# A hybrid attention and expert kernel: one written order from the end of the attention on, and all second experts dense

## The chip, the cores and the metric

The kernel runs on one core of one Trainium2 chip. A core has engines that run side by side, each taking its own instructions in order: TensorE (PE in the profile, with its weight loads as PEld), VectorE (DVE), ScalarE (ACT), GpSimd (POOL) and SyncE (SP), which here only issues transfers. The metric is the device time of one execution in microseconds; of several executions the median is given.

## The reference

`x` has four batches of 1024 tokens with 128 features. All is float32. Four stages follow each other, each added to `x` after a layer norm:

```python
x = x + attn_a(layernorm(x))      # 16 heads of 64, causal, softmax with the row's maximum over all columns
x = x + ffn(layernorm(x))         # 32 experts of 128x128, the two best of each token
x = x + attn_b(layernorm(x))      # linear attention: cumulative sums of k*v and k, 16 heads of 8
x = x + ffn(layernorm(x))         # the same experts and router again

# ffn
rw = softmax(x @ router_w.T)                       # (tokens, 32)
vals, idx = top_k(rw, 2)
w_masked = zeros_like(rw).at[tokens, idx].set(vals)
out = sum over e of (x * w_masked[:, e]) @ expert_weights[e]
```

A token needs only its two best experts. A kernel may compute all 32 for every token, with a weight of zero for the other 30 ("dense"), or sort the tokens by expert first and compute only what is needed ("sparse").

## The kernel before

The residual stream `x_sb` stays on the chip as 32 chunks of 128 tokens, 8 to a batch. Four neighbouring chunks are called a quad here.

**The attention** (lines 487 to 845) works through 4 batches x 8 pairs of heads in an order that is written out by hand: within `tc.manual_schedule()`, each engine gets its instructions in the order in which the program emits them. Beside it runs the *sparse* first expert layer of batches 0, 1 and 2: the generator `experts` (from line 214), of which `beside` takes a step in each slot. It sorts tokens with counts on POOL, scatters rows to DRAM with indirect transfers, reads them back sorted, multiplies tile by tile, and writes results to DRAM. Then come 16 indirect transfers per batch (line 449) that POOL issues and that add rows of the results into `x_sb`. They lie in `queue` and are taken out one at a time. The sparse layer of batch 2 is nearly done when the attention ends: one of its 16 additions has been issued then, and 15 are left.

**The stages behind the attention.** The weights of all 32 experts are loaded to `we_sb` (line 856, four transfers of 512 KB). `moe` (line 860) is the dense expert layer, used twice: as "f" for the first expert layer of batch 3 (quads 6 and 7), and as "s" for the second expert layer of batches 1 to 3 (quads 2 to 7). For one quad it does

1. `normed_T` (line 130): statistics unless `known`, the normalised rows `xn` (DVE), four transposes (PE), a copy `xnT` (ACT),
2. the router: four small products `pl` (L886), maximum, `exp`, sum, the two best by `max` and `match_replace` (L892 to L912, mainly DVE), giving the weights `w`,
3. for each of 4 chunks 8 products `pe` of 128x512 (L922, four experts each). Groups 1, 4 and 6 go to ACT: four multiplications by the weight into a tile `t` (L930). The other five go to DVE: four instructions each that multiply and add into `x_sb` (L937). POOL adds the three `t` (L944) and folds the sum (L945, L946); DVE adds that to `x_sb` (L871, in `settle`).

A product lies in one of five PSUM banks (`ps_e`), so PE can be five products ahead of the engine that empties them.

**Who orders what.** `moe` is outside the manual sections: there the compiler's planner orders the instructions of each engine by its own estimate of when each is ready, and it may put them among those of a neighbouring stage, the linear attention included. Between two products `moe` calls `between`: in "f" this is `fill`, which steps the generator `prepare` (L970; norm, projections and feature maps of a quad for the linear attention) for quads 0 and 1, and after turn 8 takes the left-over transfers from `queue`. In "s" it is `pieces`, which steps the *sparse* second expert layer of batch 0 (`experts` with the prefix `s0`; its sums come into tiles `y_s` and are added to `x_sb` by DVE, L476 and L481).

**The linear attention** (from L1071) is manual. For each chunk `u`, POOL forms the products `kv` (L1085), PE sums them over the chunk (`cum`, L1103) and carries them on (L1111), DVE multiplies by the queries (`m`, L1123) and reduces (`num`, L1132), and `finish` transposes, projects and adds to `x_sb` (L1152). `ahead` steps `prepare` for quads 2 to 7.

Of the kernel before, what the change touches and what calls it, by code (L numbers as in the profile page):

```python
# [15 lines left out]
P = 128  # L16
# [4 lines left out]
def hybrid_kernel(  # L21
# [107 lines left out]

    def normed_T(pool, xnp, c0, n, nm, known=None):  # L130

        mv, rstd = known or statistics(c0, n, nm)
        xn = xnp.tile([P, n, D], F32, tag=f"xn{n}", bufs=8 // n, name=f"xn_{nm}")
        xnT = xnp.tile([P, n * P], F32, tag=f"xnT{n}", name=f"xnT_{nm}")
        for c in range(n):
            nc.vector.tensor_scalar(
                xn[:, c, :], x_sb[:, c0 + c, :], mv[:, c, 0:1], rstd[:, c : c + 1],
                ALU.subtract, ALU.mult,
            )
        for g in range(0, n, 4):  # L140
            pt = pool.tile([P, 512], F32, tag="ps1", name=f"pxn_{nm}_{g}")
            for c in range(4):
                nc.tensor.transpose(pt[:, c * P : (c + 1) * P], xn[:, g + c, :], ident)
            nc.scalar.copy(xnT[:, g * P : (g + 4) * P], pt)
        return xnT
# [711 lines left out]
    TB = 12  # L857
    ACT_GROUPS = (1, 4, 6)

    def moe(nm_, store, first=0, between=None, known=(), lag=0):  # L860
        with ExitStack() as ph:
            xnp = ph.enter_context(tc.tile_pool(name=f"xnp{nm_}", bufs=2, reuse_waits="tile"))
            mp = ph.enter_context(tc.tile_pool(name=f"mp{nm_}", bufs=3, reuse_waits="tile"))
            ps_1 = ph.enter_context(tc.tile_pool(name=f"mps1{nm_}", bufs=3, space=PSUM, reuse_waits="tile"))
            ps_e = ph.enter_context(tc.tile_pool(name=f"mpse{nm_}", bufs=5, space=PSUM, reuse_waits="tile"))
            due = []

            def settle(keep):
                while len(due) > keep:
                    xs, s, done = due.pop(0)  # L870
                    nc.vector.tensor_tensor(xs, xs, s[:, :D], ALU.add)  # L871
                    if store and done is not None:
                        b, r = divmod(done, NB)
                        nc.sync.dma_start(
                            out=out_v[b, :, r : r + 4, :], in_=x_sb[:, done : done + 4, :]
                        )

            for q in range(first, NT // 4):
                nm = f"{nm_}_{q}"
                c0 = q * 4  # L880
                xnT = normed_T(
                    ps_1, xnp, c0, 4, f"m{nm}", known[q - first] if known else None
                )
                pl = ps_1.tile([P, 512], F32, tag="ps1", name=f"pl_{nm}")
                for c in range(4):
                    nc.tensor.matmul(  # L886
                        pl[:, c * E : (c + 1) * E], xnT[:, c * P : (c + 1) * P], rwT,
                        start=True, stop=True,
                    )
                plv = pl[:, : 4 * E].rearrange("p (c e) -> p c e", c=4)  # L890
                mx = small.tile([P, 4], F32, tag="mx", name=f"mx_{nm}")
                nc.vector.tensor_reduce(mx, plv, AX.X, ALU.max)  # L892
                ex = mp.tile([P, 4, E], F32, tag="ex", name=f"ex_{nm}")
                nc.vector.tensor_tensor(
                    ex, plv, mx.unsqueeze(2).to_broadcast([P, 4, E]), ALU.subtract
                )
                nc.scalar.activation(ex, ex, AF.Exp)
                sm = small.tile([P, 4], F32, tag="sm", name=f"sm_{nm}")
                nc.vector.tensor_reduce(sm, ex, AX.X, ALU.add)
                nc.vector.reciprocal(sm, sm)  # L900
                tp, rwx = top[q % 2]
                nc.vector.tensor_tensor(
                    rwx[:, :, 0:E], ex, sm.unsqueeze(2).to_broadcast([P, 4, E]), ALU.mult
                )
                m8 = small.tile([P, 4, 8], F32, tag="m8", name=f"m8_{nm}")
                for c in range(4):
                    nc.vector.max(m8[:, c, :], rwx[:, c, 0:E])
                nc.vector.tensor_copy(tp[:, :, 0:2], m8[:, :, 0:2])
                w = mp.tile([P, 4, E + 6], F32, tag="w", name=f"w_{nm}")
                for c in range(4):  # L910
                    nc.vector.match_replace(w[:, c, :], tp[:, c, :], rwx[:, c, :], 0.0)
                nc.vector.tensor_tensor(  # L912
                    w[:, :, 0:E], rwx[:, :, 0:E], w[:, :, 0:E], ALU.subtract
                )
                for c in range(4):
                    xs = x_sb[:, c0 + c, :]
                    parts = []
                    for g in range(E // 4):
                        if between:
                            between(ps_1)  # L920
                        pe = ps_e.tile([P, 512], F32, tag="e", name=f"pe_{nm}_{c}_{g}")
                        nc.tensor.matmul(  # L922
                            pe, xnT[:, c * P : (c + 1) * P],
                            we_sb[:, 4 * g : 4 * g + 4, :].rearrange("p e d -> p (e d)"),
                            start=True, stop=True,
                        )
                        if g in ACT_GROUPS:
                            t = mp.tile([P, 512], F32, tag="t", bufs=TB, name=f"t_{nm}_{c}_{g}")
                            for e in range(4):
                                nc.scalar.mul(  # L930
                                    t[:, e * D : (e + 1) * D], pe[:, e * D : (e + 1) * D],
                                    w[:, c, 4 * g + e : 4 * g + e + 1],
                                )
                            parts.append(t)
                        else:
                            for e in range(4):
                                nc.vector.scalar_tensor_tensor(  # L937
                                    xs, pe[:, e * D : (e + 1) * D],
                                    w[:, c, 4 * g + e : 4 * g + e + 1], xs,
                                    ALU.mult, ALU.add,  # L940
                                )
                    s = parts[0]
                    for t in parts[1:]:
                        nc.gpsimd.tensor_tensor(s, s, t, ALU.add)  # L944
                    nc.gpsimd.tensor_tensor(s[:, :256], s[:, :256], s[:, 256:], ALU.add)  # L945
# [102 lines left out]
    def fill(pool):  # L1048
# [3 lines left out]
        if turn[0] in (4, 18):  # L1052
            preps.append(prepare(len(preps), pool))
# [12 lines left out]
    for p in preps:  # L1066
        for _ in p:
            pass
# [162 lines left out]
```

## Time and profile before

| | us |
|---|---|
| median of 3 runs | 2033.25 (2030.45 to 2037.73) |
| the profiled execution's own time | 2037.51 |
| its span, first to last instruction | 2035.8 |
| attention, to the first transfer of `we_sb` | 0 to 1482 |
| "f", dense first experts of batch 3 | 1482 to 1596.5 (first `cum`) |
| linear attention | 1596.5 to 1785.7 (last addition to `x_sb`) |
| "s", second experts | 1785.7 to 2035.8 |

In the 250 us from 1786 on PE is busy for 213.0 us, DVE for 184.0, POOL for 135.9 and ACT for 102.6. Times in the rows are microseconds from the start of the span. A row of the timeline gives start, length, engine, line, what is written from what, how many instructions were merged, and in brackets how long the engine had been idle and what ended that. Neighbouring instructions of one engine overlap in it, so the length of one is more than what it adds: sixteen instructions of L937 took 4.22 us together, where one alone shows as 0.34.

### The profile page before, as it was taken

Reading aid. Unit: us, or ns where it says so; the run is one execution under the profiler, and the core shown is the slowest. Engines: PE = TensorE matmul, PEld = TensorE weight load, DVE = VectorE, ACT = ScalarE, POOL = GpSimd, SP = SyncE. Lnnn points to the kernel's source line nnn. Section 1 sums busy time; section 2 is a strip of 40 time slices with the busy share of each in tenths; the row PEclk is TensorE's granted clock in tenths of the full one; section 3 lists DMA queues with packets and bytes.
Section 4 is the critical chain, followed back from the end, with each engine's and each line's share of the span. In section 5 each row is a group of like instructions: output and inputs, shape, how many; then the busy total and the mean of one; then the engine's idle time right before and its main releaser. Section 6 shows DMA issues by size and latency. Waiting matters only on the chain.

```text
span 2035.8 us, 33636 instructions
## 1 busy us (share of the span) xinstructions
PE 1890.7 (93%) x10066; PEld 1052.5 (52%) x10066; DVE 1482.9 (73%) x4467; ACT 1234.6 (61%) x3889; POOL 1139.5 (56%) x2080
## 2 busy tenths in 40 slices
PE   6999999999999999999999999999958898987898
PEld 3555555555555655555565555556633454543443
DVE  5777776776787677778767676777547678966788
ACT  4766666676677566766766676776526466334344
POOL 3444445444665476556745854675476566655644
PEclk9999999999999999999999999999979999997999
DMA  7000000000003310000131100003230000004300
GB/s 214 1 1 1 1 1 1 1 1 1 1 13 93 92 22 10 1 1 5 54 107 45 18 1 1 1 17 111 80 82 0 0 0 1 0 1 123 101 11 11
DMA packets 111875, 62.54 MB, mean 31 GB/s; under 512 B 5552, under 2 KB 110160, under 8 KB 111568
## 3 DMA queue, kind: packets, MB, share of 16 engines
q1 hardware_dynamic: 101936, 50.43, 8.7%
q0 software_dynamic: 9472, 8.40, 2.1%
q8 instruction: 82, 1.34, 0.3%
q10 hardware_dynamic: 288, 1.57, 0.2%
q14 instruction: 97, 0.79, 0.1%
HBM read 35.60 MB, written 24.77 MB: 30 GB/s over the span
## 4 chain that ended last, share of the span: by engine, by line
PE 64%; DVE 12%; ACT 10%; POOL 9%; issue 3%; DMA 1%; ACTq 0%; SPq 0%; POOLq 0%; DVEq 0%
PE s L598 19%; PE po L704 10%; PE pt L687 10%; PE pe_s L922 6%; DVE nmx L607 5%; ACT p L632 3%; PE pw L719 3%; PE pk L547 3%; POOL x_sb L449 2%; ACT pT L691 2%; PE pe L430 2%; PE pv L561 2%; PE cum L1103 1%; ACT p L637 1%; PE pe_f L922 1%
## 5 line engine op out<-in xcount | busy, mean ns | idle before, releaser
L607 DVE TENSOR_REDUCE nmx<-s 128x2 f32<-128x1024 f32 x512 | 604.5, 1219 | 218.5 <-PE s L598 217.8
L632 ACT ACTIVATE p<-s,nmx 128x512 f32<-128x512 f32 (+3 forms) x640 | 361.2, 575 | 311.8 <-DVE nmx L607 264.5
L598 PE MATMUL s<-kT,qT 64*128 64x512 f32 x2048 | 518.0, 619 | 8.0 <-ACT p L632 4.5
L674 POOL TENSOR_SCALAR p<-p,f,ri 128x512 f32<-128x512 f32 (+3 forms) x768 | 503.8, 673 | 0.9 <-issue 0.6
L687 PEld LDWEIGHTS pt<-ident,p 128*128 128x128 f32 x2304 | 249.9, 141 | 219.1 <-issue 91.1
L687 PE MATMUL pt<-ident,p 128*128 128x128 f32 x2304 | 335.9, 282 | 24.4 <-POOL rs L652 7.1
L691 ACT COPY pT<-pt 128x512 f32<-128x512 f32 (+3 forms) x768 | 324.4, 510 | 11.9 <-PE pt L687 9.6
L656 POOL TENSOR_TENSOR rs<-rs,f 128x2 f32<-128x2 f32 x256 | 52.1, 204 | 438.5 <-ACT f L623 409.1
L704 PE MATMUL po<-pT,va 128*64 128x256 f32 (+1 forms) x2560 | 291.1, 365 | 0.6 <-DVE oT L711 0.6
L598 PEld LDWEIGHTS s<-kT,qT 64*128 64x128 f32 x2048 | 173.3, 185 | 195.4 <-issue 94.2
L637 ACT ACTIVATE p<-s,nmx 128x128 f32<-128x128 f32 x512 | 180.7, 366 | 107.3 <-DVE nmx L607 104.6
L704 PEld LDWEIGHTS po<-pT,va 128*64 128x64 f32 x2560 | 167.0, 136 | 97.2 <-issue 32.6
L922 PE MATMUL pe_s<-we_sb,xnT_ms 128*128 128x512 f32 x384 | 186.4, 630 | 22.9 <-DVE x_sb L937 16.4
L937 DVE SCALAR_TENSOR_TENSOR x_sb<-pe_s,w_s,x_sb 128x128 f32<-128x128 f32 x480 | 141.4, 343 | 19.2 <-PE pe_s L922 14.6
L645 DVE SCALAR_TENSOR_TENSOR p<-p,qtri 128x128 f32<-128x128 f32 x512 | 144.9, 310 | 7.0 <-ACT p L637 3.9
L652 POOL TENSOR_TENSOR rs<-rs 128x2 f32<-128x2 f32 x192 | 43.9, 229 | 186.7 <-DVE ri L665 186.7
L632 ACT ACTIVATION_READ_ACCUMULATOR p<-s,nmx 128x1 f32 x640 | 139.0, 217 | 0.0
L930 ACT ACTIVATE t_s<-pe_s,w_s 128x128 f32<-128x128 f32 x288 | 82.2, 369 | 92.5 <-PE pe_s L922 75.5
L922 PEld LDWEIGHTS pe_s<-we_sb,xnT_ms 128*128 128x128 f32 x384 | 72.2, 199 | 116.3 <-issue 37.4
L944 POOL TENSOR_TENSOR t_s<-t_s,t_s 128x512 f32<-128x512 f32 x48 | 60.9, 1269 | 81.4 <-ACT t_s L930 81.1
L724 DVE TENSOR_TENSOR x_sb<-pw,x_sb 128x128 f32<-128x128 f32 x128 | 36.9, 289 | 79.8 <-PE pw L719 79.7
L719 PE MATMUL pw<-wo_sb,oT 128*128 128x128 f32 x512 | 84.5, 289 | 1.8 <-DVE x_sb L724 1.0
(302 smaller groups left out, 2669.5 us busy)
## 6 DMA issues: line engine op xcount, KB each, us to landing
xs<-xs_d SPq DMA_DIRECT2D x33, 256.0 KB, 3.1
ys_d<-ys SPq DMA_DIRECT2D x33, 256.0 KB, 2.4
we<-_ffn_expert_weights_dram SPq DMA_DIRECT2D x24, 256.0 KB, 3.6
xs_d<-zero SPq DMA_DIRECT2D x2, 3008.0 KB, 17.9
we<-_ffn_expert_weights_dram SPq DMA_DIRECT2D x45, 64.0 KB, 1.8
xs_s<-xs_d SPq DMA_DIRECT2D x11, 256.0 KB, 3.6
ys_d<-ys_s SPq DMA_DIRECT2D x11, 256.0 KB, 3.4
we_sb<-_ffn_expert_weights_dram SPq DMA_DIRECT2D x4, 512.0 KB, 6.0
```

The source lines that it names most:

```text
L598: nc.tensor.matmul(st[:, h, :], self.qT[rows, self.ib * P : (self.ib + 1) * P], self.kT[rows, j * 512 : (j + 1) * 512], start=True, stop=True,
L607: nc.vector.tensor_reduce(self.nmx[:, i, :], self.s[i], AX.X, ALU.max, negate=True)
L632: nc.scalar.activation(self.p[h][:, at : at + m * P], self.s[i][:, h, : m * P], AF.Exp, bias=bias, accum_out=self.rs[:, i, h : h + 1],)
L637: nc.scalar.activation(self.p[h][:, at + m * P : at + (m + 1) * P], self.s[i][:, h, m * P : (m + 1) * P], AF.Exp, bias=bias,)
L645: nc.vector.scalar_tensor_tensor(d, d, 1.0, qtri, ALU.mult, ALU.mult, accum_out=self.rs[:, 2, h : h + 1])
L674: nc.gpsimd.tensor_scalar(w, w, self.f[:, i, h : h + 1], self.ri[:, h : h + 1], ALU.mult, ALU.mult,)
L687: nc.tensor.transpose(pt[:, c * P : (c + 1) * P], self.p[h][:, (g + c) * P : (g + c + 1) * P], ident,)
L691: nc.scalar.copy(self.pTs[h][:, g : g + m, self.col : self.col + P], pt[:, : m * P].rearrange("p (c i) -> p c i", c=m),)
L704: nc.tensor.matmul(po[h * DH : (h + 1) * DH, c0:256], va[:, jb, h, :], pTs[h][:, jb, c0:], start=(jb == 0), stop=(jb == n - 1),)
L719: nc.tensor.matmul(pw[:, :P], oTs[i][:, c * P : (c + 1) * P], wo_sb[:, pr, :], start=(i == 0), stop=(i == len(prs) - 1),)
L922: nc.tensor.matmul(pe, xnT[:, c * P : (c + 1) * P], we_sb[:, 4 * g : 4 * g + 4, :].rearrange("p e d -> p (e d)"), start=True, stop=True,)
L937: nc.vector.scalar_tensor_tensor(xs, pe[:, e * D : (e + 1) * D], w[:, c, 4 * g + e : 4 * g + e + 1], xs, ALU.mult, ALU.add,)
```

## The change

The whole rest of the kernel from the attention's end on is put under one `manual_schedule`. `normed_T` and `moe` are replaced by two functions. `routed` is a generator that does steps 1 and 2 of a quad in pieces, with empty steps between pieces that depend on another engine. `dense` does step 3 for a list of quads; after each product it takes one step of `routed` of the next quad and calls `beside(turn)`. POOL's first two additions now follow as soon as their tiles are written, and `settle(2)` stands behind the fourth product of each chunk (before: behind the eighth, with a lag of 0 in "f" and 3 in "s").

- "f": the first `routed` is stepped together with `prepare` of quad 0. Then `fill` steps `prepare` of quad 0 at even turns and of quad 1 at odd ones, and takes one left-over transfer at every fourth turn. What remains is taken behind the last product. The tiles `t` have 9 buffers here.
- linear attention: its pools now wait for their predecessors tile by tile. From chunk 24 on, each round takes two steps of `routed` for quad 0.
- "s": all 8 quads are dense; the sparse layer of batch 0 with its transfers is gone. `t` has 12 buffers. Statistics of quads 1 to 7 are taken within `dense`, one quad ahead.

```diff
+    ctx.enter_context(tc.manual_schedule())
+    def routed(q, nm, pool, known=None):
+        if known is None:
+            for c in range(4):
+                nc.vector.bn_stats(st[:, c, :], x_sb[:, c0 + c, :])
+                nc.vector.bn_aggr(mv[:, c, :], st[:, c, :])
+                yield
+            nc.vector.tensor_scalar_add(ve, mv[:, :, 1], LN_EPS)
+            nc.gpsimd.tensor_tensor(rstd, ve, mhalf[:, :4], ALU.pow)
+            yield
+            yield
+            yield
...
+        for c in range(4):
+            nc.vector.tensor_scalar(xn[:, c, :], ...)
+            if c == 1:
+                yield
+        yield
+        yield
+        yield
+        for c in range(4):
+            nc.tensor.transpose(pt[:, c * P : (c + 1) * P], xn[:, c, :], ident)
+        nc.scalar.copy(xnT, pt)
+        yield
+        yield
+        yield
+        yield
+            nc.tensor.matmul(
...
+        yield
+        yield
+        nc.vector.tensor_reduce(mx, plv, AX.X, ALU.max)
...
+        nc.scalar.activation(ex, ex, AF.Exp)
+        yield
+        yield
+        nc.vector.tensor_reduce(sm, ex, AX.X, ALU.add)
...
+        yield
+            nc.vector.max(m8[:, c, :], rwx[:, c, 0:E])
+        nc.vector.tensor_copy(tp[:, :, 0:2], m8[:, :, 0:2])
+        yield
+            nc.vector.match_replace(w[:, c, :], tp[:, c, :], rwx[:, c, :], 0.0)
+        yield
+        nc.vector.tensor_tensor(w[:, :, 0:E], rwx[:, :, 0:E], w[:, :, 0:E], ALU.subtract)
+    def dense(nm_, qs, store, pool, mp, ps_e, known, beside):
...
+                        parts.append(t)
+                        if len(parts) > 1:
+                            nc.gpsimd.tensor_tensor(parts[0], parts[0], t, ALU.add)
...
+                    if g == 3:
+                        settle(2)
+                    next(nxt, None)
+                    beside(turn)
+                    turn += 1
...
+        def fill(turn):
+            next(preps[turn % 2], None)
+            if turn % 4 == 3:
+                if queue:
+                    queue.pop(0)()
+                on()
+        for _ in routed(qs[0], f"f_{qs[0]}", ps_f, known[0]):
+            next(preps[0], None)
+        dense("f", qs, False, ps_f, mp, ps_e, known, fill)
+        for p in preps:
+            for _ in p:
+                pass
+        while sides or queue:
+            if queue:
+                queue.pop(0)()
+            on()
...
-        lp = ph.enter_context(tc.tile_pool(name="lp", bufs=3))
+        lp = ph.enter_context(tc.tile_pool(name="lp", bufs=3, reuse_waits="tile"))
...
+            if u == NT - 8:
+                first = routed(qs[0], f"s_{qs[0]}", ps_1)
+            next(first, None)
+            next(first, None)
...
-    for b, r in enumerate((room,)):
-        sides.append(experts(b, f"s{b}", banks, queue, r, came))
-    moe("s", True, NB // 4, pieces, lag=3)
+    dense("s", qs, True, ps_s, mp, ps_e, [None] * len(qs), lambda turn: None)
```

## The prediction

> **What bounds the kernel now.** I first cut the span at the stage borders and read the busy times of each stretch (columns: stretch, length, busy us and instructions of PE, PEld, DVE, ACT, POOL, then PE clock, DMA share, GB/s).
>
> ```profile
> 1482.00:1513.00 31.00, 10.77 (x26) 5.58 (x26) 13.71 (x73) 4.88 (x14) 25.81 (x23) 0.66 0.60 127
> 1513.00:1594.00 81.00, 68.21 (x150) 28.67 (x150) 55.41 (x179) 48.15 (x142) 47.54 (x60) 0.90 0.02 3
> 1594.00:1786.00 192.00, 169.85 (x532) 96.45 (x532) 157.87 (x376) 98.94 (x241) 123.13 (x94) 0.94 0.00 1
> 1786.00:1930.00 144.00, 117.93 (x397) 60.50 (x397) 95.03 (x371) 57.83 (x181) 84.58 (x99) 0.90 0.27 77
> 1930.00:2036.00 106.00, 95.10 (x224) 40.77 (x224) 88.92 (x337) 44.80 (x156) 51.34 (x56) 0.95 0.05 13
> ```
>
> "f" wastes its first 31 us: PE works 10.8 of them, POOL 25.8. The timeline there says why:
>
> ```profile
> 1501.45 0.18 DVE L978 BATCH_NORM_AGGREGATE mv_l<-st_l 128x2 f32<-128x6 f32 x1 [8.59 <-POOL nb_l L985]
> ...
> 1510.67 1.26 ACT L992 ACTIVATE xn_l<-x_sb,nb_l,rstd_l 128x128 f32<-128x128 f32 x3 [5.52 <-POOL nb_l L986]
> ...
> 1513.00 8.42 PE L922 MATMUL pe_f<-we_sb,xnT_mf 128*128 128x512 f32 x12 [7.32 <-ACT t_f L930]
> ```
>
> The planner put the 15 left-over additions of L449 first on POOL (1485 to 1516). The small norm instructions of `prepare` stand between them, DVE and ACT stand waiting for those ahead of the weights and multiplications of "f", and PE waits for a bank until 1513. In "s" and at its end the PE rows are:
>
> ```profile
> 1834.17 2.07 PE L922 MATMUL pe_s<-we_sb,xnT_ms 128*128 128x512 f32 x2 [5.11 <-DVE x_sb L937]
> ...
> 1930.28 6.28 PE L922 MATMUL pe_s<-we_sb,xnT_ms 128*128 128x512 f32 x8 [3.68 <-DVE x_sb L937]
> ...
> 1965.48 14.00 PE L922 MATMUL pe_s<-we_sb,xnT_ms 128*128 128x512 f32 x32 [0.44 <-ACT t_s L930]
> 1979.31 0.97 PE L886 MATMUL pl_s<-rwT,xnT_ms 128*128 128x32 f32 x8
> 1980.12 7.11 PE L922 MATMUL pe_s<-we_sb,xnT_ms 128*128 128x512 f32 x16
> ```
>
> While the sparse layer runs beside it, PE is held up by several us at a time; once that is done, PE is nearly full. Two records make one product, so 16 products run from 1965.48 to 1979.31 (0.86 each), and `pl` adds 0.81.
>
> **"f", part by part.** Nothing of its work is removed; the order changes. The additions now come one per four products, after the dense work has begun. The start, followed by rows: `xn` begins at 1484.4 as before; with the statistics of `prepare` between its pieces DVE needs 2.7 us, then POOL 1.9 for the norm (0.20, 1.01, 0.20 and 0.23 plus gaps, the rows at 1699.6, where no transfer is between; between transfers it took 0.7 to 1.6 each). ACT then works in the written order, with what PE feeds it: four `xn_l` 1.65, two copies 1.2, PE's cold `pj` 1.2, four sets of `pj` copies at 0.83 with short waits for PE 5.1, exponential and copy 1.9, router exponential 0.3, sigmoid and logarithm with their table loads 4.1: about 1504.4. DVE has the weights by then (router rows 1.5, `y` 1.2, `match_replace` and difference 1.0 behind the exponential). Against 1511.8 for ACT's first multiplication before.
>
> From there POOL is the fullest: additions of eight chunks 8 x (1.27 + 1.27 + 0.72 + 0.45 + gaps) = 31.9; 15 transfers at 1.75 each, the spacing of one that stands between other work in the attention (1.15 to the next instruction, which is then 0.5 longer) = 26.3; the feature maps of two `prepare` 10.0, `gt` 1.3, one norm 1.9, and 2.5 idle until DVE has quad 1's statistics. Sum 73.9, end 1578.3, then the first `kv` 2.1: the first `cum` at 1580.5. PE needs only 59 x 0.86 + 3.9 (`pj` and transposes of quad 1) + 1.3 = 56, so it waits for POOL. Before, `cum` came at 1596.5: 16 earlier. Waits in order can only add: DVE's `kq` at turn 10 waits for POOL, behind it stand the DVE groups whose banks PE needs; 9 buffers of `t` limit how far POOL may lag. I take 2 off: **-14**, with ends of 0 and -16 while POOL bounds.
>
> **The linear attention.** Its DVE stream loses the planner's insertions: 28 pairs of statistics of the second experts, and four `ve` whose rows there are 1.00, 1.42, 1.02 and 1.69. The pairs lie in latency gaps: from `num` to `o` it took 2.34 with one and 2.25 without, so 0.1 each. Together 8, of which the chain that ended last shows about half on it: -5. Quad 0's router (5.6 on DVE, below) comes in; its statistics fall into the same gaps, `ve`, `xn` and PE's 1.3 don't: +2. Net **-3**, between +4 and -8.
>
> **The junction.** From the last `x_sb` addition (1785.7) to DVE's first L937 (1792.5) it took 6.8, all router of quad 2. Now that router ends with the loop. DVE can start some 5 earlier, PE 2.5 earlier (`pe` began at 1788.0): **-3**.
>
> **"s".** The sparse layer goes: 94 + 47 small matrix instructions on PE, 32 indirect transfers in POOL's queue with its counting, and in SP's queue 12 reads, 12 writes and 23 loads of weights. Two dense quads come, with two stores of 256 KB on SP, which at 3 us each per 30 us have room. Per quad:
>
> - PE: 4 x 8 x 0.857 + 0.81 + 0.44 (four transposes between two rows of 1943.14 and 1943.58) = 28.7.
> - DVE: 80 of L937 at 0.263 (16 in 4.22) and four L871 at 0.21 = 21.8; router: statistics 1.6, `xn` 1.1, the rest at spacings of the rows from 1551.5 to 1556.2, 2.9: 5.6. Sum 27.4.
> - ACT 4 x 12 x 0.286 + 0.9 = 14.6, POOL 4 x 4.0 + 1.0 = 17: both hidden under PE.
>
> PE and DVE are thus almost equal, and what blocks DVE counts. The rows (group view, 1786 to 2036; columns count, busy, mean ns, idle):
>
> ```profile
> L944 POOL TENSOR_TENSOR t_s<-t_s,t_s 128x512 f32<-128x512 f32 x48 | 60.9, 1269 | 81.4 <-ACT t_s L930 81.1
> ...
> L871 DVE TENSOR_TENSOR x_sb<-x_sb,t_s 128x128 f32<-128x128 f32 x24 | 8.9, 370 | 6.6 <-POOL t_s L946 6.5
> ...
> L912 DVE TENSOR_TENSOR w_s<-rwx,w_s 128x128 f32<-128x128 f32 x6 | 3.4, 564 | 0.0
> ...
> L908 DVE COPY top<-m_s 128x8 f32<-128x8 f32 x6 | 2.7, 452 | 0.0
> ```
>
> L912 was 0.284 and L908 0.17 where undisturbed, `ve` 0.17 against about 1.0. By these means a quad loses 0.28 + 0.28 + 0.8 + 4 x 0.09 = 1.7: DVE 29.1. The Trainium skill ("SBUF — State Buffer", section "Who interferes with whom") speaks against the change here: a DVE copy or `tensor_scalar` in a two-port mode, or a DVE instruction with two SBUF inputs, and a reading POOL instruction exclude each other wholly, and the later one waits. As an estimate from that: twelve such instructions per quad (`ve`, four `xn`, L908, `rwx`, L912, four L871), POOL busy 17 of 29 us, half of a 1.27 left when met, 12 x 0.58 x 0.63 = 4.4: DVE 31.8, and "s" 17 longer than by the trace's means. I take the rows, since they were measured with the same POOL additions running, plus 0.6 for waits of a fixed order: 29.7 a quad. Bounds: 28.7 (PE alone), 31.8.
>
> An in-order step waits where its maker is late: ACT's `xnT` copy waits for PE's transposes, and behind it stand ACT's multiplications and so PE's banks; `xn` waits for POOL's `rstd`, which stands behind up to 4 us of additions with three products (2.6) of lead. PE stops when five banks are full. These are in the 0.6.
>
> From first to last product: 8 x 29.7, less 2 for quad 0's router, = 235.6, against 240.8 before (1788.0 to 2028.8): **-5**. The tail of 7.0 behind the last product (POOL 2.5, DVE 0.3, the store) stays.
>
> **Sum.** -14 - 3 - 3 - 5 = -25 of a span of 2035.8: 2010.8, or 2012.5 of the profiled execution's own 2037.51. The median lies 4.3 below that execution: 2033.25 - 25 = **2008**.
>
> **Rivals.**
> 1. *The forecast*, 0.50: 1998 to 2021.
> 2. *POOL doesn't bound "f"*, 0.10. If transfers overlap with additions, PE sets the end: 1504.4 + 56 + 4 + 2.1 = 1566.5, 14 further: 1994. Against it: 15 x 1.75 was measured in order.
> 3. *"f" gains nothing*, 0.15. DVE waits for POOL's queue at `kq`, `settle` and the banks, and POOL in turn for DVE; `cum` stays at 1596.5: 2022. For it: DVE waited 5.1 for `kq` in "f" before.
> 4. *All is given back*, 0.10. 25 / 8 = 3.1 more per quad, i.e. 32.8: 2033. The planner's order was then as good.
> 5. *Slower*, 0.15. DVE is locked out by POOL in "s". From 3.9 per quad on (33.6) it is over 0.3% slower. The longest rows bound it: `ve` 1.69, L908 1.06, L912 1.23, four L871 at 1.30; each time all of these cost 1.5 + 0.9 + 0.9 + 4 x 1.0 = 7.3, which gives 2008 + 8 x 5.6 = 2053 (1.7 being counted already). The middle between that point (2039) and this end is 2046. Against it: after 1966 DVE was busy 85% with such additions beside it, and PE still 97%.
>
> That the change does nothing can't be: two quads and a sparse layer change places.
>
> **Range.** 0.3% (6.1 us) is about what a measurement of this kernel can tell. Faster holds 1, 2 and 3: 0.75; same 4: 0.10; slower 5: 0.15. Eight in ten: from 1993, which leaves out half of rival 2, to 2038, which leaves out most of rival 5. The likeliest case's own range is 1998 to 2021.
>
> **What would show it.** "f": no DVE or ACT wait of several us on `nb_l`, transfers spread to about 1575, first `cum` near 1582, POOL over 85% busy between. Linear attention: 186 us, no `ve` but one. "s": 32 chunks at about 7.4 us each; PE over 93% busy. It is wrong if PE waits for DVE by over a us at each router, if L871, L908 or `ve` average above 0.8 us, or if POOL is idle in "f" while PE waits.

## The result, and the profile after

The changed kernel takes 2094.19 us (median of 4 runs, 2089.88 to 2095.76) against 2033.24 us on the same chip: 1.0294 times as long, with an interval of 1.027 to 1.0318. The forecast was 2008, its range 1993 to 2038. It was wrong in sign and outside the range. The profiled execution took 2089.88 us, its span 2088.1, which is 52.3 more than the span of before.

The stages, in columns of the same kind as those shown of before (stretch, length, busy us of PE, PEld, DVE, ACT and POOL, then clock, DMA share, GB/s), in the order "f", linear attention, "s":

```profile
1481.00:1588.00 107.00, 78.17 (x179) 31.13 (x178) 83.14 (x252) 54.45 (x158) 74.43 (x68) 0.90 0.16 29
1588.00:1772.00 184.00, 166.02 (x529) 93.94 (x529) 150.57 (x317) 94.69 (x228) 115.71 (x87) 0.97 0.00 1
1772.00:2088.00 316.00, 259.34 (x610) 104.94 (x609) 282.56 (x924) 117.37 (x402) 125.89 (x135) 0.97 0.02 7
```

In the last stage DVE is busy for 283 of 316 us, PE for 259. From border to border, with the times of the first `cum`, of the first `cum` of the last chunk ("last" in the table), of the first product of "s" and of the end of its last:

| part | before | after | difference | forecast |
|---|---|---|---|---|
| to the first `cum` | 1596.5 | 1588.7 | -7.8 | -14 |
| linear attention, first to last `cum` | 182.3 | 181.0 | -1.3 | -3 |
| junction, last `cum` to first product of "s" | 9.3 | 6.6 | -2.6 | -3 |
| "s", first to last product | 240.8 | 302.8 | +62.1 | -5 |
| tail | 7.0 | 9.0 | +1.9 | 0 |
| sum | | | +52.3 | -25 |

So everything was lost in "s": 302.8 us for 8 quads is 37.9 each, where 29.7 was forecast. The clock is no rival: the granted clock is 0.97 in this stage, and before it was 0.90 and 0.95 in the two parts of "s". PE, which ran 16 products without a break before, now stands still behind every two or three in such stretches (two records are one product):

```profile
1925.39 2.84 PE L949 MATMUL pe_s<-we_sb,xnT_s 128*128 128x512 f32 x6 [1.23 <-ACT t_s L957]
1928.67 2.84 PE L949 MATMUL pe_s<-we_sb,xnT_s 128*128 128x512 f32 x6 [0.43 <-ACT t_s L957]
1931.94 2.84 PE L949 MATMUL pe_s<-we_sb,xnT_s 128*128 128x512 f32 x6 [0.43 <-ACT t_s L957]
```

The brackets name ACT, but ACT is busy for 117 of 316 us and itself waits for PE, 136 us in all. The chain that ended last, in the stretch from 1776 to 2079, names the one that is slow (shares of the chain by line):

```profile
by line: DVE x_sb L966 55.6%; PE pe_s L949 16.2%; issue 6.8%; ACT t_s L957 3.3%; DVE xn_s L868 2.4%; DVE st_s L853 1.9%; DVE mv_s L854 1.7%; DVE rwx L907 1.7%; DVE w_s L918 1.6%; DVE x_sb L931 1.5%; DVE m_s L913 1.1%; PE pl_s L887 1.1%; PE 
```

L966 is the old L937: multiply a product by the weight and add it into `x_sb`. Here are its rows in both kernels. Before, the first in "s" and the second in "f":

```profile
1985.48 4.22 DVE L937 SCALAR_TENSOR_TENSOR x_sb<-pe_s,w_s,x_sb 128x128 f32<-128x128 f32 x16
...
1540.73 5.18 DVE L937 SCALAR_TENSOR_TENSOR x_sb<-pe_f,w_f,x_sb 128x128 f32<-128x128 f32 x13
```

After:

```profile
1906.51 3.12 DVE L966 SCALAR_TENSOR_TENSOR x_sb<-pe_s,w_s,x_sb 128x128 f32<-128x128 f32 x8
1909.55 1.30 DVE L931 TENSOR_TENSOR x_sb<-x_sb,t_s 128x128 f32<-128x128 f32 x1
1910.77 4.53 DVE L966 SCALAR_TENSOR_TENSOR x_sb<-pe_s,w_s,x_sb 128x128 f32<-128x128 f32 x12
...
1923.90 6.15 DVE L966 SCALAR_TENSOR_TENSOR x_sb<-pe_s,w_s,x_sb 128x128 f32<-128x128 f32 x16
```

Sixteen take 4.22 us in the one and 6.15 in the other, without an idle gap in either. One of them lasts about as long in both, 343 and 349 ns in the mean (group view of "s": count, busy us, mean ns, idle us):

```profile
L937 DVE SCALAR_TENSOR_TENSOR x_sb<-pe_s,w_s,x_sb 128x128 f32<-128x128 f32 x480 | 141.4, 343 | 19.2 <-PE pe_s L922 14.6
...
L966 DVE SCALAR_TENSOR_TENSOR x_sb<-pe_s,w_s,x_sb 128x128 f32<-128x128 f32 x640 | 221.6, 349 | 25.4 <-PE pe_s L949 2.1
```

So the spacing differs: (4.22 - 0.34) / 15 = 0.259 us, less than one lasts, so that neighbours overlap; and (6.15 - 0.35) / 15 = 0.387, more than one lasts. The second row of before, in "f", shows that the slow spacing was there already: 13 in 5.18 us.

What differs is the neighbour. `x_sb` of a chunk is read and written by each of its 20 multiply-adds. Counted in the order of DVE's instructions in the two programs: of 480 multiply-adds of "s" before, 82 stand directly behind one of their own chunk, 297 behind one of another chunk (the planner mixed two chunks), 101 behind something else. After, it is 542, 24 and 74 of 640. In "f" it goes from 76, 72 and 12 to 141, 6 and 13.

Some DVE instructions with inputs in SBUF alone got longer too, by POOL or not: the addition of the sum takes 606 ns where it took 370, `xn` 394 where it took 338 and `rwx` 729 where it took 304 (group view, 1772 to 2088):

```profile
L931 DVE TENSOR_TENSOR x_sb<-x_sb,t_s 128x128 f32<-128x128 f32 x32 | 19.2, 606 | 0.0
...
L868 DVE TENSOR_SCALAR xn_s<-x_sb,mv_s,rstd_s 128x128 f32<-128x128 f32 x28 | 9.9, 394 | 0.0
...
L907 DVE TENSOR_TENSOR rwx<-ex_s,sm_s 128x128 f32<-128x128 f32 x8 | 5.8, 729 | 0.3
```

**Theory:** a multiply-add that reads the chunk which the one just before it wrote begins only when that one is finished, 0.387 instead of 0.259 us apart. 542 x 0.128 = 69 us of DVE in "s", 8.7 a quad. **Rivals:** POOL's additions hold DVE up (L931 at 606 ns); the dense quads are too dear in any order; PE waits for the order of its banks, whatever DVE does.

### The profile page after: what moved, and what is told of

Its sections match the earlier page's. It is cut to its first block, busy times and chain, and to the rows that moved or that the text cites. A ratio compares the mean times of both kernels' runs of the same rounds, so it can differ in the third digit from the quotient of the medians.

```text
span 2088.1 us, 33601 instructions
## 1 busy us (share of the span) xinstructions
PE 1931.7 (93%) x10049; PEld 1050.2 (50%) x10049; DVE 1587.2 (76%) x4627; ACT 1244.7 (60%) x3945; POOL 1120.9 (54%) x2038
## 3 DMA queue, kind: packets, MB, share of 16 engines
q8 instruction: 82, 1.34, 0.3%
## 4 chain that ended last, share of the span: by engine, by line
PE 57%; DVE 25%; ACT 9%; POOL 5%; issue 3%; DMA 0%; ACTq 0%; DVEq 0%; SPq 0%; POOLq 0%
PE s L581 18%; DVE x_sb L966 11%; PE po L687 10%; PE pt L670 10%; DVE nmx L590 6%; ACT p L615 3%; PE pw L702 3%; PE pk L530 3%; PE pe_s L949 2%; ACT pT L674 2%; PE pe L413 2%; PE cum L1144 2%; PE cum L1152 2%; ACT p L620 1%; PE pv L544 1%
## 5 line engine op out<-in xcount | busy, mean ns | idle before, releaser
L949 PE MATMUL pe_s<-we_sb,xnT_s 128*128 128x512 f32 x512 | 244.8, 618 | 30.1 <-ACT t_s L957 29.6
L966 DVE SCALAR_TENSOR_TENSOR x_sb<-pe_s,w_s,x_sb 128x128 f32<-128x128 f32 x640 | 221.6, 349 | 25.4 <-PE pe_s L949 2.1
L957 ACT ACTIVATE t_s<-pe_s,w_s 128x128 f32<-128x128 f32 x384 | 109.4, 367 | 147.5 <-PE pe_s L949 135.6
L949 PEld LDWEIGHTS pe_s<-we_sb,xnT_s 128*128 128x128 f32 x512 | 93.5, 195 | 170.6 <-ACT t_s L957 81.6
L963 POOL TENSOR_TENSOR t_s<-t_s,t_s 128x512 f32<-128x512 f32 x64 | 81.0, 1266 | 168.8 <-ACT t_s L957 168.7
```

Of the source, the lines that this page charges most:

```text
L949: nc.tensor.matmul(pe, xnT[:, c * P : (c + 1) * P], we_sb[:, 4 * g : 4 * g + 4, :].rearrange("p e d -> p (e d)"), start=True, stop=True,)
L966: nc.vector.scalar_tensor_tensor(xs, pe[:, e * D : (e + 1) * D], w[:, c, 4 * g + e : 4 * g + e + 1], xs, ALU.mult, ALU.add,)
```

## The experiments

Each is timed against the kernel before on the same chip. Line numbers shift a little between kernels: the multiply-add, L966 in the changed kernel, is L970, L971 or L972 in some rows below.

**Two chunks together in "s".** No instruction is added or left out. The work on two chunks is interleaved: products, multiplications on ACT and POOL's additions come in pairs, and the multiply-adds alternate between the two.

```diff
-            for c in range(4):
+            if store:
+                for c in (0, 2):
...
+                        for k in range(2):
+                            pe = ps_e.tile([P, 512], F32, tag="e", ...)
+                            nc.tensor.matmul(...)
+                            pes.append(pe)
...
+                            for e in range(4):
+                                for k in range(2):
+                                    stt(k, e)
```

> The changed kernel with two chunks of a quad taken together in s alone: products of both, then the multiply-adds of L966 alternate between the two chunks. Theory (a multiply-add that reads what the one before it wrote follows at 0.38 us, one of another chunk at 0.263, and DVE sets the pace of s): a run of eight takes about 2.1 us in place of 3.1, DVE needs about 30 us per quad in place of 37.8, s shortens by some 60 us, and the time is about 2034 (2026 to 2044). Rival (DVE is held by waits of the written order or by POOL's port, whatever the multiply-adds follow): the spacing or the time stays, 2080 to 2096.

And its control, which takes two chunks together as well, but the multiply-adds in blocks of four. It differs from the alternating kernel in these two lines alone:

```diff
-                            for e in range(4):
-                                for k in range(2):
+                            for k in range(2):
+                                for e in range(4):
                                     stt(k, e)
```

> As the run with two chunks together in s, with the same products, banks, additions and router pieces, but the four multiply-adds of one chunk stand in a block before the four of the other. Theory of the dependent spacing: each block of four takes 1.5 us as in the changed kernel, and the time is 2085 to 2100. Rival (what the pairing changes is the look-ahead of PE or the lag of POOL's sums): as fast as with alternating multiply-adds, 2026 to 2044.

Measured: 2037.86 us (ratio 1.0011, 1.0004 to 1.0018) for the alternating one and 2087.89 (1.0253, 1.0235 to 1.027) for the blocks. Both came out as the theory expected. "s" takes 247.8 us in the first, 31.0 a quad, and 301.6 in the second. DVE's rows, alternating:

```profile
1900.65 2.15 DVE L972 SCALAR_TENSOR_TENSOR x_sb<-pe_s,w_s,x_sb 128x128 f32<-128x128 f32 x8
...
1903.96 6.28 DVE L972 SCALAR_TENSOR_TENSOR x_sb<-pe_s,w_s,x_sb 128x128 f32<-128x128 f32 x24
```

and in blocks:

```profile
1900.46 2.92 DVE L972 SCALAR_TENSOR_TENSOR x_sb<-pe_s,w_s,x_sb 128x128 f32<-128x128 f32 x8
...
1910.91 4.35 DVE L972 SCALAR_TENSOR_TENSOR x_sb<-pe_s,w_s,x_sb 128x128 f32<-128x128 f32 x12 [2.59 <-PE pe_s L952]
```

Twenty-four in 6.28 are 0.258 apart; twelve in 4.35 are 0.36, one in four of them at a change of chunk. The same instructions, products and banks, with neighbours exchanged, are 50 us apart. That decides for the neighbour, and against the order of PE's banks: the stage of the alternating kernel gives back 55.0 of the 62.1 us. One thing goes along with it: alternating neighbours also read different PSUM banks. The next kernel keeps that apart, since there the four neighbours of a product read the same bank.

**Two sums within a chunk.** A second test of the same cause without pairs: odd multiply-adds go to a second sum, which DVE adds at the end.

```diff
+                if store:
+                    acc = mp.tile([P, D], F32, tag="acc", bufs=3, ...)
+                    nc.gpsimd.memset(acc, 0.0)
...
+                            to = acc if store and e % 2 else xs
                             nc.vector.scalar_tensor_tensor(
-                                xs, pe[:, e * D : (e + 1) * D],
-                                w[:, c, 4 * g + e : 4 * g + e + 1], xs,
+                                to, pe[:, e * D : (e + 1) * D],
+                                w[:, c, 4 * g + e : 4 * g + e + 1], to,
...
+                if store:
+                    nc.vector.tensor_tensor(xs, xs, acc, ALU.add)
```

> The changed kernel with its written order of chunks and products in s, but the multiply-adds of a chunk go in turn into x_sb and into a second sum (cleared by POOL, added to x_sb by DVE at the chunk's end), so that none reads what the one just before it wrote. Theory of the dependent spacing: 80 multiply-adds at 0.263 in place of 0.38 save 9.4 us per quad, less 1.2 to 3 for the four added additions, so s shortens by 50 to 60 us where PE allows it, and the time is 2032 to 2048. Rival (it is the mixing of two chunks in PE's and ACT's order that helps): 2080 or more.

Measured: 2057.01 us (1.0103, 1.008 to 1.0125), 9 us later than the end of what was expected. The spacing is as expected (starts 0.26 apart), with neighbours in the same bank:

```profile
1905.23 0.34 DVE L970 SCALAR_TENSOR_TENSOR acc_s<-pe_s,w_s,acc_s 128x128 f32<-128x128 f32 x1
1905.49 0.34 DVE L970 SCALAR_TENSOR_TENSOR x_sb<-pe_s,w_s,x_sb 128x128 f32<-128x128 f32 x1
1905.75 0.34 DVE L970 SCALAR_TENSOR_TENSOR acc_s<-pe_s,w_s,acc_s 128x128 f32<-128x128 f32 x1
```

But the group view shows waits that I had not counted:

```profile
L970 DVE SCALAR_TENSOR_TENSOR x_sb<-pe_s,w_s,x_sb 128x128 f32<-128x128 f32 x317 | 107.8, 340 | 11.8 <-PE pe_s L952 11.7
L970 DVE SCALAR_TENSOR_TENSOR acc_s<-pe_s,w_s,acc_s 128x128 f32<-128x128 f32 x316 | 107.8, 341 | 12.0 <-POOL acc_s L949 12.0
...
L981 DVE TENSOR_TENSOR x_sb<-x_sb,acc_s 128x128 f32<-128x128 f32 x31 | 12.6, 406 | 0.8
```

DVE waits 12.0 us for POOL to clear the second sum, which stands in POOL's queue behind the additions, and 11.7 for PE. The new additions cost 12.6 for 31 of 32, 1.6 a quad, which is within the 1.2 to 3 that were expected.

**POOL's additions left out of "s".** This kernel leaves out the sum of the three `t` and its folding, so that of the twelve experts of a chunk that go to ACT only one is added to `x_sb` (the expectation below says four). It serves for timing alone.

```diff
-                        if len(parts) > 1:
+                        if len(parts) > 1 and not store:
                             nc.gpsimd.tensor_tensor(parts[0], parts[0], t, ALU.add)
...
-                nc.gpsimd.tensor_tensor(s[:, :256], s[:, :256], s[:, 256:], ALU.add)
-                nc.gpsimd.tensor_tensor(s[:, :D], s[:, :D], s[:, D : 2 * D], ALU.add)
+                if not store:
+                    nc.gpsimd.tensor_tensor(s[:, :256], s[:, :256], s[:, 256:], ALU.add)
+                    nc.gpsimd.tensor_tensor(s[:, :D], s[:, :D], s[:, D : 2 * D], ALU.add)
```

> The changed kernel without POOL's additions of the t tiles in s; it leaves out two of the three ACT groups from the sum of each chunk and adds only the first four experts of the first. The rival of the prediction (DVE is locked out by POOL in s) prices what this removes: if it is the main cost, more than 30 us come back. Theory of the dependent spacing: only the longer rows go back to their short lengths, L931 0.61 to 0.28 in 32 and rwx 0.73 to 0.29 in 8, so 12 to 18 us, time 2075 to 2083.

Measured: 2073.79 us (1.0195, 1.0178 to 1.0212), 1 us below what was expected and 20.4 below the changed kernel.

```profile
L966 DVE SCALAR_TENSOR_TENSOR x_sb<-pe_s,w_s,x_sb 128x128 f32<-128x128 f32 x636 | 220.2, 349 | 27.0 <-PE pe_s L949 4.2
...
L868 DVE TENSOR_SCALAR xn_s<-x_sb,mv_s,rstd_s 128x128 f32<-128x128 f32 x28 | 8.3, 339 | 0.0
L931 DVE TENSOR_TENSOR x_sb<-x_sb,t_s 128x128 f32<-128x128 f32 x29 | 8.1, 281 | 0.0
```

L931 is back at 281 ns, `xn` at 339. So the hold-up is real, but its price is known only roughly. The 20.4 us between the medians are 2.5 a quad. In the profiled executions "s" takes 292.7 us here, 302.8 in the changed kernel and 306.5 in the kernel with early transfers below, whose "s" is the same: that is 10 to 14 us, or 1.3 to 1.7 a quad, and the tail is 3.4 shorter. The multiply-adds keep their spacing, and the kernel is still 40 us slower than before: POOL alone doesn't explain it.

**Less work on DVE: a fourth group on ACT in "s".** `t` has 16 buffers instead of 12 for it.

```diff
-                    if g in ACT_GROUPS:
+                    if g in ((1, 3, 4, 6) if store else ACT_GROUPS):
```

> The changed kernel with four of eight groups on ACT in s (1, 3, 4, 6; 16 buffers of t), so 16 multiply-adds per chunk on DVE in place of 20. Theory (DVE with its dependent spacing is the bound of s): 4 x 1.52 us less per quad, about 32 us per quad, s some 45 us shorter, time 2045 to 2062. Rival (waits of the order bound it): less than 15 us gained.

Measured: 2056.57 us (1.0103, 1.0086 to 1.012), as expected; "s" takes 33.3 a quad. Taking a fifth of the multiply-adds from DVE shortens the stage by 36.5 us, though PE has nothing less to do: DVE bounds it.

**The dense quads in the planner's order.** The kernel before, with all eight second quads dense and no sparse layer behind the attention.

```diff
-    for b, r in enumerate((room,)):
-        sides.append(experts(b, f"s{b}", banks, queue, r, came))
-    moe("s", True, NB // 4, pieces, lag=3)
+    moe("s", True, 0, None, lag=3)
```

> The kernel before with only one part of the change: the second experts of batch 0 are dense too, in the planner's order, and the sparse layer beside them is gone. Theory (the planner's order mixes two chunks, and the dense quads are not what costs): s at about 30 us per quad as in the last 60 us of the kernel before, so 8 x 30 - 2 = 238 against 241, and the time is 2020 to 2040. Rival (the two more dense quads cost what the change lost): 2080 or more.

Measured: 2042.03 us (1.0036, 1.0023 to 1.0049), 2 us above what was expected. "s" takes 244.5 us, 30.6 a quad, with 54 of 640 multiply-adds behind one of their own chunk.

```profile
1786.00:2030.00 244.00, 236.43 (x596) 104.69 (x595) 215.81 (x864) 114.02 (x398) 120.44 (x129) 0.99 0.03 8
```

PE is busy for 236 of 244 us. So the two more dense quads in place of a sparse layer cost 7 us and gain nothing; the other 52 us of the changed kernel come with its written order.

**Pairs in "f" as well.** The alternating order in both stages, with 12 buffers of `t` in "f".

```diff
-        mp = ph.enter_context(tc.tile_pool(name="mpf", bufs=9, reuse_waits="tile"))
+        mp = ph.enter_context(tc.tile_pool(name="mpf", bufs=12, reuse_waits="tile"))
```

> Two chunks together in f as well as in s (12 buffers of t in f). If DVE's dependent spacing bounds f too, f shortens by up to 160 x 0.12 = 19 us and the time is near 2020. If POOL bounds f, as predicted, only the wait of the first kv for DVE and part of POOL's idle time go: 2 to 5 us, time 2033 to 2036.

Measured: 2032.85 us (0.9996, 0.9987 to 1.0005): the same as before, and what was expected if POOL bounds "f".

**Transfers early, alone and with pairs.** Eight of the 15 left-over transfers go where POOL stood idle, ahead of the first multiply-adds of "f".

```diff
-        for _ in routed(qs[0], f"f_{qs[0]}", ps_f, known[0]):
+        for k, _ in enumerate(routed(qs[0], f"f_{qs[0]}", ps_f, known[0])):
             next(preps[0], None)
+            if k in (3, 4, 5, 6, 7, 10, 11, 12) and queue:
+                queue.pop(0)()
```

> The changed kernel, with eight of the fifteen left-over transfers of the attention taken while the first router of the expert layer f is stepped, five behind the first norm of POOL and three behind its addition to gt, instead of between the products; POOL stood idle there for 10.0 and 5.4 us. Theory: POOL's queue from 1505 on bounds f in the changed kernel (15 x 1.6 to 1.75 of 74 us), so eight fewer behind that point take 8 x 1.6 = 13 us off it; then DVE is next, with 160 multiply-adds at about 0.38 = 61 us plus router and sums of about 10 from 1511 on, end near 1582, so the first carry of the linear attention comes 4 to 8 us earlier and the whole takes 2086 to 2091 instead of 2094. Rival (the first products wait for banks and DVE already, POOL only follows): no change, 2092 to 2096. Second rival: transfers ahead of gt and of the feature maps delay those, since DVE's and ACT's norms wait for POOL as before the change: slower, 2097 or more.

> Two chunks taken together in both expert layers (multiply-adds alternate between them) and eight left-over transfers taken early. Theory: with alternating multiply-adds DVE needs 160 x 0.263 = 42 us in f, so POOL alone bounds it (first carry 1582.2 with pairs alone), and 13 us off its queue pass on until PE's 57 us from about 1508 bind: first carry 1570 to 1575, whole 2020 to 2027 against 2033 before and for pairs alone. Rival (POOL doesn't bound f even then): 2031 to 2035.

Measured: the change with early transfers 2093.46 us (1.0291, 1.0275 to 1.0307); pairs in both stages with early transfers 2024.9 us (0.9956, 0.9942 to 0.9969). The first is what the rival expected (no change), the second what the theory did. From the last `rstd_mf` row on POOL, which ends the statistics ahead of "f" in each kernel, to the first `cum`:

| | one chunk at a time | pairs |
|---|---|---|
| transfers between the products | 105.1 | 100.9 |
| eight of them early | 104.9 | 94.9 |

Before, it was 112.5. Kernels with the same "f" as the changed one lie between 103.8 and 105.1, so that early transfers alone show no gain. Pairs alone gain 4.2 us (they come with 12 buffers of `t` instead of 9), and together the two give 10.3: each alone frees one engine and finds the other close behind. With early transfers alone, POOL has idle time in "f" and the end doesn't move:

```profile
1568.71 1.27 POOL L963 TENSOR_TENSOR t_f<-t_f,t_f 128x512 f32<-128x512 f32 x1 [4.07 <-ACT t_f L957]
...
1577.68 1.26 POOL L963 TENSOR_TENSOR t_f<-t_f,t_f 128x512 f32<-128x512 f32 x1 [3.88 <-ACT t_f L957]
```

while DVE stands in a closed row of multiply-adds:

```profile
1564.71 7.75 DVE L966 SCALAR_TENSOR_TENSOR x_sb<-pe_f,w_f,x_sb 128x128 f32<-128x128 f32 x20
1572.39 0.28 DVE L931 TENSOR_TENSOR x_sb<-x_sb,t_f 128x128 f32<-128x128 f32 x1
1572.59 7.77 DVE L966 SCALAR_TENSOR_TENSOR x_sb<-pe_f,w_f,x_sb 128x128 f32<-128x128 f32 x20
```

The combination is the fastest of all: 0.44% faster than the kernel before, 69 us faster than the changed one.

**Two attempts to relieve DVE further, both failed.** Pairs in both stages and a fourth group on ACT in "s":

> Two chunks together in f and s, and four of eight groups on ACT in s. DVE then needs 4 x (16 x 0.263 + 0.28) + 8 = 26 us per quad, ACT 19 and POOL 21, so PE with 28.7 is the bound: s near 8 x 29.3 = 234 in place of 247, time 2017 to 2027, below the kernel before. If PE is not the bound behind DVE (waits of the order), less than 5 us against the run with pairs in both.

Measured: 2060.98 us (1.0132, 1.0115 to 1.0149), 28 slower than without the fourth group, where a gain was expected. `t` has 16 buffers in "s" here as well. Its groups in "s":

```profile
L961 ACT ACTIVATE t_s<-pe_s,w_s 128x128 f32<-128x128 f32 x512 | 137.1, 410 | 61.6 <-PE pe_s L951 29.8 <-POOL t_s L989 21.0 <-POOL t_s L988 7.0
...
L868 DVE TENSOR_SCALAR xn_s<-x_sb,mv_s,rstd_s 128x128 f32<-128x128 f32 x28 | 34.6, 1295 | 6.6 <-POOL rstd_s L859 6.6
```

With three full additions per chunk POOL is busy for 160 of 278 us, and ACT waits 28 us for buffers that POOL frees late. `xn` takes 1295 ns, against 582 without the fourth group. A full POOL alone doesn't do that: in the kernel with a fourth group and without pairs it is busy for 164 of 265 us, and `xn` takes 402. What differs is how often the two meet: without the fourth group one `xn` in four takes about 1.3 us and the others 0.34, with it nearly all take 1.3. The clock is lower as well. The stage without the fourth group and with it (clock third from the end):

```profile
1772.00:2020.00 248.00, 232.47 (x594) 102.12 (x592) 224.99 (x906) 110.45 (x398) 121.98 (x131) 1.00 0.03 8
...
1771.00:2049.00 278.00, 251.75 (x598) 109.97 (x597) 228.34 (x775) 143.90 (x528) 160.24 (x162) 0.94 0.02 7
```

Behind the four transposes of a router, which now wait for `xn` one by one, four products take 4.9 to 6.2 us instead of 3.6. Over the stage `xn` lasts 20 us longer in all and these products 13; "s" is 30 us longer, though DVE has a fifth fewer multiply-adds.

Pairs with early transfers, and `xn` of "s" formed on ACT:

```diff
+            nc.vector.scalar_tensor_tensor(nb, mv[:, :, 0], -1.0, rstd, ALU.mult, ALU.mult)
...
-            nc.vector.tensor_scalar(
-                xn[:, c, :], x_sb[:, c0 + c, :], mv[:, c, 0:1], rstd[:, c : c + 1],
-                ALU.subtract, ALU.mult,
-            )
+            if known is None:
+                nc.scalar.activation(
+                    xn[:, c, :], x_sb[:, c0 + c, :], AF.Identity,
+                    scale=rstd[:, c : c + 1], bias=nb[:, c : c + 1],
+                )
```

> As the one with pairs and early transfers, and in the second layer the normalised rows come from ACT (scale and bias, with one more small DVE instruction per quad) instead of four DVE instructions per quad. Theory: those four average 0.58 in the layer beside POOL's additions, and PE waits for their transposes 5.4 us in all; DVE loses 4 x 0.58 - 0.2 = 2.1 us per quad, ACT gains 4 x 0.4 = 1.6 and has room; but with pairs PE is 94% busy there, so no more than about 6% of 248 us can come: 4 to 10 us faster than the same kernel with these rows on DVE, 2012 to 2020. Rival: ACT's multiplications, for whose banks PE waits already (8.6 us), are held up by four rows more: no gain or up to 5 us slower.

Measured: 2044.28 us (1.0051, 1.0038 to 1.0065), 19 slower than with `xn` on DVE. The rival had the direction, but not the size. PE's rows at one router:

```profile
1876.68 0.71 PE L887 MATMUL pxn_s<-ident,xn_s 128*128 128x128 f32 x2
1879.49 0.85 PE L887 MATMUL pxn_s<-ident,xn_s 128*128 128x128 f32 x2 [2.10 <-ACT xn_s L871]
1880.14 5.02 PE L959 MATMUL pe_s<-we_sb,xnT_s 128*128 128x512 f32 x8
```

Two `xn` stand on ACT behind eight multiplications, and PE waits 2.10 us in the middle of its transposes. Behind that break four products take 5.02 us. At the same place without `xn` on ACT the break is 0.76 and they take 3.61:

```profile
1876.05 0.33 PE L879 MATMUL pxn_s<-ident,xn_s 128*128 128x128 f32 x1 [0.76 <-DVE xn_s L868]
1876.21 3.61 PE L951 MATMUL pe_s<-we_sb,xnT_s 128*128 128x512 f32 x8
```

The granted clock over those 10 us is 0.83 with `xn` on ACT and 1.00 without:

```profile
1876.00:1886.00 10.00, 7.77 (x23) 3.81 (x22) 3.41 (x15) 6.55 (x21) 4.99 (x5) 0.83 0.00 1
...
1876.00:1886.00 10.00, 9.95 (x30) 5.06 (x31) 7.62 (x29) 3.84 (x14) 4.79 (x6) 1.00 0.00 0
```

The break recurs at every router, with 2.10 each time. From one router's products to the next a quad takes 34.66 us in three of six cases here (34.25 to 36.15 in the others) and 31.44 without `xn` on ACT; the longer break (1.34) and the slower products behind it (1.41) are 2.75 of these 3.2. Whether the clock falls because of the break was not tested by itself.

## Why the prediction was wrong

**The step that failed: "80 of L937 at 0.263 (16 in 4.22)".** That row is right, but it belongs to an order in which two chunks alternate. The written order takes one chunk at a time, and there the spacing is 0.387: 31 us for the 80 instead of 21.0. The alternating kernel gives back 55.0 of 62.1 us, 6.9 a quad of the 8.2 by which a quad exceeded the forecast. The prediction counted these instructions and took one duration, without asking to which neighbour that duration belongs, although the row of 13 in 5.18 us stood in the profile of before.

The Trainium skill ("VectorE: DVE Perf Modes", section "The DRAIN you can't avoid") says that the next DVE instruction starts only when the pipe is empty, and that a semaphore between two costs nothing extra, measured there with copies. These runs don't bear that out for this instruction: independent neighbours start 0.259 us apart, each lasting 0.34, and dependent ones 0.387. The same section adds that an instruction which isn't held starts earlier, which fits the independent ones. In both orders the program lets these instructions wait on DVE's own semaphore, for the one just before in the one order and for the one before that in the other. What the 0.128 consists of, that wait or the pipe, the runs don't tell.

**The loss to POOL's port, 1.7 a quad.** Leaving the additions out gained 1.3 to 1.7 a quad by the traces of "s" and 2.5 by the medians, so the term was about right. The rule of the skill that was weighed against it ("SBUF — State Buffer", section "Who interferes with whom") gave 4.4 as an estimate; the measured value lies nearer to the rows of the trace. (The "17 longer than by the trace's means" is counted from 29.7; from the means alone, 29.1, it is 22.) With pairs and three additions per chunk, though, the rule's kind of loss appears in full, `xn` at 1295 ns. The price isn't a mean to carry along: with a POOL as full, but without pairs, `xn` took 402.

**"f", -14.** It gave -7.8. The start came as worked out (the feature maps at 1505.4, forecast 1504.4). DVE's wait of 8.6 us for `nb_l` is gone, and ACT's second one is 1.7 instead of 5.5. POOL worked without a break from 1515.7 to 1584.0, where 1578.3 was forecast. Of these 5.7 us, 1.0 is the start, 2.8 is idle time ahead of quad 1's norm (5.3, where 2.5 was allowed), and 1.9 is spread over the work. The transfers were not dearer than forecast: the next row starts 1.09 later and then takes 1.24 instead of 0.73, together 1.6, where 1.75 was counted:

```profile
1513.27 0.20 POOL L1016 TENSOR_TENSOR rstd_l<-mv_l,epsn 128x4 f32<-128x4 f32 x1 [5.31 <-DVE mv_l L1011]
...
1539.04 1.56 POOL L432 DMA_INDIRECT x_sb<-ys_d,row  x1 [0.15 <-issue]
1540.13 1.24 POOL L977 TENSOR_TENSOR t_f<-t_f 128x256 f32<-128x256 f32 x1
...
1586.52 4.20 POOL L1126 TENSOR_TENSOR kv<-kq,va 128x1024 f32<-128x1024 f32 x2 [2.53 <-DVE x_sb L931]
```

But "From there POOL is the fullest" was only half the reason: DVE, which I never summed for "f", has 160 x 0.387 = 62 us of multiply-adds there, is busy for 73.9 of the 83 us from 1505 on (POOL for 69.9) and ends later; `kv` waits 2.5 us for it in the last row. The table of four shows that POOL's relief alone gains nothing. My working summed POOL and PE, but not the third engine.

**Linear attention -3 and junction -3.** They gave -1.3 and -2.6. The first shows nothing: over all the kernels here that stretch takes 178.4 to 184.0 us, and the changed kernel's 181.0 and the 182.3 of before both lie inside. The junction came as said. **The tail** is 1.9 longer: behind the last product DVE still has 8 slow multiply-adds and four additions.

**The rivals.** Rival 5 had the sign, the stage and the engine, but the wrong mechanism: it needed 33.6 a quad from POOL's locks. By the run without POOL's additions these came to at most 0.8 more than counted, i.e. 30.5 a quad, which would not have made the kernel slower than before. Its bound of 35.3 a quad (29.7 + 5.6) and 2053 us was passed, by something else. Rival 2 (POOL doesn't bound "f") was true only as a statement on POOL: the end was not earlier, since DVE stood beside it.

**The signs named ahead.** PE was to be busy over 93% and was at 85% (257 of 303 us); chunks were to take 7.4 us and took 9.5. PE waited for DVE by over a us at each router of "s" (1.34 or 1.35 for `xn`), as was named. But the mean of L931, the old L871, stayed at 0.61 us in "s", that of L914, the old L908, at 0.29 and that of `ve` at 0.17, below the 0.8 that was to show rival 5: the signs for the time were there, the sign for that cause was not.

## What to carry to other kernels

A duration from a profile belongs to its neighbourhood: ahead of a change of order, find for each costly instruction what stands before it, and whether it reads what that one wrote. When an order is written out by hand for instructions that add into the same tile, let two tiles alternate; a planner may have done so unasked. And sum every engine of a stage, not only the one that looks fullest: relieving one of two engines that are nearly level can gain little (0.2 and 4.2 us in "f" here), where relieving both gained 10.3.

## What the runs showed of the hardware

- Multiply-adds of 128x128 from a product into `x_sb` on DVE: 0.259 us apart when neighbours write different chunks, 0.387 when each reads what the one before wrote; the duration of a single one hardly differs (median 340 and 351 ns). The same holds with two sums in one chunk (0.26).
- DVE instructions with inputs in SBUF alone beside POOL's additions: L931 281 ns without them, 606 in the changed kernel; `xn` 339 without, 394 in the changed kernel, 402 with one more full addition per chunk, 582 with pairs, and 1295 with both.
- Behind a break of 2.1 us between transposes, four products took 5.02 instead of 3.61 us at a granted clock of 0.83 over 10 us, where it was 1.00 with a break of 0.76.
